# A GRU scan with an expert-choice layer: bias into the sum banks by ScalarE, six banks for late sums, exponentials in an odd step

## The chip, the cores and the metric

The kernel runs on one core of a Trainium2 chip. The metric is the device time of one execution in microseconds; lower is better. TensorE (PE) does matmuls into PSUM, VectorE (DVE) and ScalarE (ACT) do elementwise work, GpSimd (POOL) copies in SBUF, and SyncE (SP) issues DMAs. [...]

## What is computed

Sixteen sequences of 256 steps with 512 features go through a GRU, one step after another. The hidden states of all 4096 tokens then go through a layer in which each of 16 experts picks its 256 best tokens; all experts share one weight matrix, so a token's output is its sum `h @ expert_w + expert_b` times the sum of the weights with which experts picked it.

```python
r = sigmoid(x @ W_ir + b + h @ W_hr + b');  z = sigmoid(...)
n = tanh(x @ W_in + b + r * (h @ W_hn + b'));  h = (1 - z) * n + z * h      # 256 steps
S = softmax(hs @ router_w + router_b)                                       # 16 experts
G, idx = top_k(S.T, 256)                                                    # per expert
y = zeros.at[idx].add(G[..., None] * (hs[idx] @ expert_w + expert_b))
out = x + y
```

## The kernel before

**Groups.** Tokens are held in 32 groups of 128 (8 steps x 16 sequences). The expert's sums of 15 early groups (0, 1, 2, and those from 4 to 27 with g % 4 < 2) are made inside the scan; those of the 17 late groups at its end and behind it.

**The scan.** `for s in range(T)` issues each step by hand (manual schedule: every engine runs its list in the order in which the code issues it). TensorE's order in a step is `h_part` for r, n, r, n, z (L458, 96 matmul records), `x_part` for the next pair of steps (L445; 24 records in even steps, 40 in odd ones), and then fillers: one *unit* of an early group's sums (`expert`, L407, four matmuls), or in two steps of every 32 the router's logits. ScalarE runs r's sigmoid (L516), two tanhs (L569), z's sigmoid zs (L570) and, in even steps alone, copies that preset the next pair's gate banks with the bias: `preset_first` (L422) right behind r, `preset_rest` (L425, at times L429, L433) behind zs. VectorE has the rest of the chain, ending in the new state hs (L590), which the next step's h_part waits for.

**Sum banks.** `ps_m` has two banks. An early group's bank is taken in `expert` at its first unit; the first of its matmuls has `start=True`, and `expert_done` (L419) adds the bias `eb` as VectorE copies the sums to SBUF, a half in each of the next two steps. Unit n runs in step n + 8, so groups begin in steps 8, 24, 40, ... 232. `idle` is one more tile of `ps_m`; `keep_clock` writes zeros into it at the kernel's start, and `begin_sums` (L112) is the four zero matmuls of one bank.

**Late sums.** `late_items` are 16 whole late groups and two halves of the last one, numbered 0 to 17 here. `late_begin` (L160) takes a bank for an item and lets ScalarE copy the bias into it; the matmuls (L137) add to that. In steps 250 and 252 (T - 6, T - 4) it begins items 0 and 1 with `fresh=True`: zero matmuls first. Item i + 2 begins when item i's matmuls have been issued; of five banks in turn, two are from `ps_m` and three from `ps_e`. `expert_for(n)` issues n parts of this work between other TensorE work.

**Softmax.** Behind the sums for step s = T - 16 = 240 to 243 come four stages for the 28 groups whose logits are done: the exponential on ScalarE (L388, with a table load before it, and a small sigmoid, L627, to load the old table again), a reduction (L390), a reciprocal (L392) and a product (L395) on VectorE.

**The tail.** Logits are transposed into `ps`; `by_bits` then looks for each expert's threshold bit by bit: VectorE counts (L658), TensorE sums the counts into `counts` (L673), VectorE decides (L676, L681). 17 bits, each with three parts of late sums on TensorE. Then `pg` (L701) sums the weights of picked tokens, `gate` (L705) is copied out, and `store` (L711, L714) scales each group's sums, adds x and issues the output's DMA, early groups first, then the late items. From the gate on (`gated`) late sums stay in their banks until their store reads them; items 0 to 7 have been copied to SBUF by then (L178). Near the end a check counts again (L780, L783).

Of the kernel before, what the change touches and what calls it, by code (L numbers as in the profile page):

```python
# [8 lines left out]
F32 = mybir.dt.float32  # L9
# [4 lines left out]
ALU = mybir.AluOpType  # L14
# [4 lines left out]
def kernel(  # L19
# [34 lines left out]
    nc = tc.nc  # L54
    B, T, D = x.shape
# [96 lines left out]
    late_done = []  # L152
    gated = []

    def late_begin(pool, fresh=False):
        g, cols = late_items[len(late_done) + len(late)]
        pe = pool.tile([P, D], F32, name="pe", tag="pe")
        if fresh:
            begin_sums(pe)
        nc.scalar.copy(pe[:, cols], eb[:, cols])  # L160
        late.append(pe)

    def late_parts():
        for i, (g, cols) in enumerate(late_items):
            pe = late[0]
            for k in range(KC):

                for part in [cols] if gated or cols != whole else halves_d:
                    late_part(g, pe, k, part)
                    if k == KC - 1 and part.stop == cols.stop:  # L170
                        if i + 2 < len(late_items):
                            late_begin(ps_m if (i + 2) % 5 < 2 else late_pool[0])
                        late.pop(0)
                        late_done.append((g, cols))
                        if gated:
                            late_sums[g, cols.start] = pe
                        else:
                            nc.scalar.copy(wide(g), pe)  # L178
                    yield
# [9 lines left out]
    with (  # L189
# [206 lines left out]

        pes = {}

        def expert(g, unit):


            quarter, k = divmod(unit, KC)
            if unit == 0:
                pes[g] = ps_m.tile([P, D], F32, name="pe", tag="pe")
            at = P * quarter
            for j in range(KC):
                nc.tensor.matmul(  # L407
                    pes[g][quadrant(j), at : at + P],
                    ht[:, g, k, quadrant(j)],
                    ewr[:, k, E + P * quarter : E + P * (quarter + 1)],  # L410
                    start=(k == 0),
                    stop=(k == KC - 1),
                    tile_position=(0, QD * j),
                )

        def expert_done(g, half):
            d = slice(HD * half, HD * (half + 1))
            to = xs[:, NG - 4, :] if g == 0 else wide(g)
            nc.vector.tensor_tensor(to[:, d], pes[g][:, d], eb[:, d], ALU.add)  # L419

        def preset_first(p):
            nc.scalar.copy(ra[p % 2], bias[:, 0:2, :])  # L422
# [42 lines left out]
                        skip_group_check=True,  # L465
                    )

        idle = ps_m.tile([P, D], F32, name="idle", tag="pe")

        def keep_clock(n):  # L470

            for _ in range(n):
                begin_sums(idle)

        with tc.manual_schedule(engines={ET.PE, ET.DVE}):
            for bank in banks:
# [23 lines left out]
        with tc.manual_schedule(engines={ET.PE, ET.Activation, ET.DVE, ET.Pool, ET.SP}):  # L500
# [4 lines left out]
            for s in range(T):  # L505
# [28 lines left out]
                if apart:  # L534
                    logits(hn[(p + 1) % 2][:, P:], (2 * c, 2 * c + 1), range(g - KC, g))
                else:
                    while units and n_units - len(units) < s - TG + 1:
                        g_, unit = units.pop(0)
                        expert(g_, unit)
                        if unit == 15:  # L540
                            done += [(g_, 0), (g_, 1)]
                if s == T - 2:
                    logits(hn[0][:, P:], range(KC), range(NG - KC, NG - 1))
                if s == T - 1:
# [60 lines left out]
                        nc.gpsimd.tensor_copy(wide(0), xs[:, NG - 4, :])  # L605
                if taken:
                    expert_done(*taken)
                if c == 3 and g + 1 < NG:
                    turn_x(g + 1, xa_next)

# [8 lines left out]
                if s == T - 2:  # L619
                    gather(NG - 1)  # L620
                if s in (T - 6, T - 4):
                    late_begin(ps_m, fresh=True)
                if T - 16 <= s < T - 12:
                    softmax(slice(0, NG - KC), s - (T - 16))
                    if s == T - 16:

                        nc.scalar.activation(seen[0:1, 0:1], seen[0:1, 0:1], AF.Sigmoid)  # L627

# [10 lines left out]
    with (  # L639
        tc.tile_pool(name="route", bufs=1) as rt,  # L640
        tc.tile_pool(name="work", bufs=2) as wk,
        tc.tile_pool(name="ps_s", bufs=1, space=bass.MemoryType.PSUM) as ps_s,
        tc.tile_pool(name="ps_c", bufs=1, space=bass.MemoryType.PSUM) as ps_c,
        tc.tile_pool(name="ps_n", bufs=1, space=bass.MemoryType.PSUM) as ps_n,
        tc.tile_pool(name="ps_e", bufs=3, space=bass.MemoryType.PSUM) as ps_e,
    ):
        late_pool.append(ps_e)
        sT = rt.tile([P, QG * P], F32, name="sT")
# [75 lines left out]
            nc.gpsimd.memset(order[:, i : i + 1], float(i + 1))  # L724

        with tc.manual_schedule(engines={ET.PE, ET.Activation, ET.DVE}):
            ps = ps_s.tile([P, KC, P], F32, name="ps", tag="s")
            ps_last = ps_n.tile([P, P], F32, name="ps_last", tag="n")
            lg_f = lg.rearrange("p e g -> p (e g)")
            for c in range(KC - 1):  # L730
                nc.tensor.transpose(ps[:, c, :], lg_f[:, c :: KC], ident)
            nc.tensor.transpose(ps_last, lg_f[:, KC - 1 :: KC], ident)
            by_block = sT.rearrange("p (q c i) -> p c q i", q=QG, c=KC)
            nc.scalar.copy(by_block[:, 0 : KC - 1], ps[:, 0 : KC - 1, :].rearrange("p c (q i) -> p c q i", q=QG))
            nc.vector.tensor_copy(by_block[:, KC - 1], ps_last.rearrange("p (q i) -> p q i", q=QG))

            expert_for(2)
            counts = ps_c.tile([P, HIGH - LOW + 1], F32, name="counts")
            top = by_bits(KNOWN, HIGH, LOW, counts, lambda bit: expert_for(3))


            nc.vector.scalar_tensor_tensor(at_least, sT, top.bitcast(F32), sT, ALU.is_le, ALU.mult)
            most = rt.tile([P, NTOP], F32, name="most")
            nc.vector.max(out=most, in_=at_least)
            spread = rt.tile([P, GH, NTOP], F32, name="spread")
            nc.vector.tensor_tensor(
                spread,
                row_of.unsqueeze(2).to_broadcast([P, GH, NTOP]),
                most.unsqueeze(1).to_broadcast([P, GH, NTOP]),
                ALU.mult,  # L750
            )
            expert_for(2)
            all_most = ps_n.tile([P, GH * NTOP], F32, name="all_most", tag="n")
            nc.tensor.matmul(all_most, same_f, spread.rearrange("p h n -> p (h n)"), start=True, stop=True)
            expert_for(3)
            room = above(counts)
            nc.vector.max(out=most, in_=all_most)
            kth = rt.tile([P, 1], F32, name="kth")
            nc.vector.scalar_tensor_tensor(
                order, order, room, most, ALU.is_equal, ALU.mult, accum_out=kth  # L760
            )
            pg = ps_s.tile([P, QG, GH], F32, name="pg", tag="s")
            for q in range(QG):
                part = slice(q * P, (q + 1) * P)
                nc.vector.scalar_tensor_tensor(at_least[:, part], sT[:, part], kth, sT[:, part], ALU.is_ge, ALU.mult)
                sum_weights(q, pg)
                if q % 2:
                    expert_for(1)
            gate = gate_of(pg)

            gated.append(True)
            items = [(g, whole) for g in early_groups] + late_items
            for i, (g, cols) in enumerate(items):
                while g in late_groups and (g, cols) not in late_done:
                    expert_for(1)

                step = i - (len(items) - 6)
                if step == 1:
                    n = ps_n.tile([P, 1], F32, name="n", tag="n")
                    nc.tensor.matmul(n, same_h, cnt, start=True, stop=True)  # L780
                elif step == 2:
                    n_wrong = ps_n.tile([1, 1], F32, name="n_wrong", tag="n")
                    nc.tensor.matmul(n_wrong, wrong, wrong, start=True, stop=True)  # L783
                store(g, late_sums.get((g, cols.start), wide(g)), gate, cols)
                if step == 0:
                    cnt = count(kth, "cnt")
                elif step == 1:
                    wrong = wk.tile([P, 1], F16, name="wrong")
                    nc.vector.tensor_scalar(wrong, n, float(TOPK), None, ALU.not_equal)
                elif step == 2:  # L790
                    nc.vector.tensor_copy(flag, n_wrong)

        again = nc.values_load(flag, min_val=0, max_val=P)
        with tc.If(again > 0):
# [14 lines left out]
            for g in range(NG):  # L809
                nc.sync.dma_start(out=xs[:, g, :], in_=x[:, g * TG : (g + 1) * TG, :])  # L810

            counts = ps_c.tile([P, 30], F32, name="counts")
            kth = by_bits(0, 29, 0, counts, lambda bit: None).bitcast(F32)


# [23 lines left out]
            nc.vector.tensor_tensor(  # L839
                rank, rank, last.unsqueeze(2).to_broadcast([P, B, QG * TG]), ALU.is_le  # L840
            )
            pg = ps_s.tile([P, QG, GH], F32, name="pg", tag="s")
            for q in range(QG):
                nc.vector.tensor_tensor(
                    by_row(at_least)[:, :, q, :], by_step(rank)[:, :, q, :], by_row(at_least)[:, :, q, :], ALU.mult
# [42 lines left out]
```

## Time and profile before

| | |
|---|---|
| median of 3 runs | 1164.77 us (1163.73 to 1165.15) |
| the profiled execution | 1164.63 us, its span 1162.8 us |
| scan: first to last r | 25.3 to 1088.0 us |
| search for the thresholds | 1094.7 to 1121.0 us |
| gate known, stores | 1126.6 to 1158.1 us |
| last output packets | between 1159 and 1160 us |
| granted TensorE clock | 1.00 from 20 us to the last matmul (0.97 from 20 to 25) |

How to read it: the scan is a fixed chain of 256 steps, so a step's time is the distance between the starts of two rows of r. In a timeline's row, the first number is the start, the second the length, both in us from the span's start; in brackets is the idle time of the engine before it, and what the profile takes for its end. Matmul records overlap, since four 32-row blocks run side by side, and "PE busy" says only that something was in flight; the rows of weight loads (PEld) show the cadence at which TensorE's list moves.

### The profile page before, as it was taken

What the parts mean: (1) busy time and instruction counts of PE and PEld (TensorE: products, weight loads), DVE (VectorE), ACT (ScalarE), POOL (GpSimd) and SP (SyncE); (2) the same over time, 40 slices, a digit from 0 to 9 for tenths busy, and PEclk for the clock granted to TensorE, in tenths of its full rate; (3) what the DMA queues carried; (4) which work ended last, traced back from release to release, by engine and by line L of the source; (5) the groups of instructions that cost most, each with busy time, mean ns of one, the idle gap of its engine ahead of it and who ended that gap; (6) DMA issues with size and microseconds to landing.
All of it is one profiled execution on the core that took longest, in us unless ns stands there. A gap on an engine that the chain in (4) does not pass through costs nothing. (4 is left out here: it accounts for less than half of the span.)

```text
span 1162.8 us, 79365 instructions
## 1 busy us (share of the span) xinstructions
PE 1147.7 (99%) x36025; PEld 1018.4 (88%) x36025; DVE 703.6 (61%) x4078; ACT 336.1 (29%) x1444; POOL 100.0 (9%) x412
## 2 busy tenths in 40 slices
PE   7999999999999999999999999999999999999998
PEld 4899999999999999999999999999999999989742
DVE  1656665666666666666665666666656666665675
ACT  0323223232323232323232322332223222243320
POOL 3000010000000000000000000000000000000000
PEclk8999999999999999999999999999999999999999
DMA  7200000000000000000000000000000000000017
GB/s 231 76 23 20 21 18 22 21 19 19 20 21 20 21 20 21 20 21 21 20 20 21 21 20 18 22 21 20 18 23 20 21 18 23 20 16 14 3 54 240
DMA packets 48854, 38.01 MB, mean 33 GB/s; under 512 B 7968, under 2 KB 40800, under 8 KB 48512
## 3 DMA queue, kind: packets, MB, share of 16 engines
q1 hardware_dynamic: 46272, 29.56, 8.7%
q8 instruction: 283, 4.64, 1.6%
q10 hardware_dynamic: 1632, 3.15, 0.8%
q14 instruction: 59, 0.48, 0.1%
q0 software_dynamic: 608, 0.19, 0.1%
HBM read 24.47 MB, written 8.39 MB: 28 GB/s over the span
## 5 line engine op out<-in xcount | busy, mean ns | idle before, releaser
L458 PE MATMUL gates<-whh,hs 128*16 128x128 f32 x24576 | 723.2, 273 | 3.4 <-DVE hs L590 3.3
L458 PEld LDWEIGHTS gates<-whh,hs 128*16 128x16 f32 x24576 | 675.6, 103 | 9.5 <-DVE hs L590 4.1
L445 PE MATMUL gates<-wih,xt 128*32 128x256 f32 (+1 forms) x8192 | 385.7, 327 | 4.0 <-DVE xt L258 4.0
L445 PEld LDWEIGHTS gates<-wih,xt 128*32 128x32 f32 x8192 | 256.0, 110 | 65.9 <-DVE xt L258 4.3
L516 ACT ACTIVATE r<-gates 128x128 f32<-128x128 f32 x256 | 71.1, 278 | 614.1 <-PE gates L458 614.1
L520 DVE COPY seen<-r 1x1 f32<-1x1 f32 x256 | 36.3, 142 | 330.2 <-ACT r L516 330.2
L569 ACT ACTIVATE t<-t 128x64 f32<-128x64 f32 x512 | 102.9, 248 | 131.6 <-DVE t L567 131.6
L576 DVE STREAM_TRANSPOSE nT<-t 128x64 f32<-128x64 f32 x512 | 100.3, 234 | 49.0 <-ACT t L569 49.0
L579 DVE STREAM_TRANSPOSE zT<-zs 128x64 f32<-128x64 f32 x512 | 121.6, 237 | 0.2 <-issue 0.2
L590 DVE TENSOR_TENSOR hs<-v,nT 128x32 f32<-128x32 f32 x512 | 101.6, 198 | 21.7
L587 DVE TENSOR_TENSOR v<-u,zT 128x32 f32<-128x32 f32 x512 | 104.5, 204 | 8.8
L407 PE MATMUL pe<-ewr,ht 128*32 128x128 f32 x1920 | 97.0, 273 | 0.0
L565 DVE TENSOR_TENSOR t<-r,gates 128x64 f32<-128x64 f32 x512 | 89.7, 217 | 0.0
L567 DVE TENSOR_TENSOR t<-t,gates 128x64 f32<-128x64 f32 x512 | 88.4, 214 | 0.0
L407 PEld LDWEIGHTS pe<-ewr,ht 128*32 128x32 f32 x1920 | 63.6, 110 | 17.4
L582 DVE TENSOR_TENSOR u<-hs,nT 128x32 f32<-128x32 f32 x512 | 78.3, 153 | 0.0
L570 ACT ACTIVATE zs<-gates 128x128 f32<-128x128 f32 x256 | 71.0, 277 | 0.0
L137 PE MATMUL pe<-ewr,ht 128*32 128x256 f32 (+1 forms) x848 | 64.5, 442 | 0.5 <-ACT pe L160 0.5
L617 POOL COPY xa<-hs 32x1 f32<-32x1 f32 x120 | 21.4, 179 | 478.2 <-DVE hs L590 297.4
L333 POOL COPY ht<-hs 128x128 f32<-128x128 f32 (+1 forms) x128 | 46.8, 396 | 160.9 <-DVE hs L590 153.1
L249 POOL COPY xs<-hs 1x1 f32<-1x1 f32 x128 | 22.7, 178 | 338.5 <-DVE hs L590 333.5
L137 PEld LDWEIGHTS pe<-ewr,ht 128*32 128x32 f32 x848 | 25.9, 109 | 27.0 <-issue 16.8
(102 smaller groups left out, 310.1 us busy)
## 6 DMA issues: line engine op xcount, KB each, us to landing
xs<-in_x_dram SPq DMA_DIRECT2D x128, 64.0 KB
xa<-in_x_dram SPq DMA_DIRECT2D x248, 32.0 KB
out_dram<-xs SPq DMA_DIRECT2D x31, 256.0 KB
wih<-in_L_cond_W_ih_dram SPq DMA_DIRECT2D x3, 512.0 KB
wih<-in_L_cond_W_ih_dram ACTq DMA_DIRECT2D x3, 512.0 KB
whh<-in_L_cond_W_hh_dram SPq DMA_DIRECT2D x3, 512.0 KB
whh<-in_L_cond_W_hh_dram ACTq DMA_DIRECT2D x3, 512.0 KB
ewr<-in_L_ffn_expert_w_dram SPq DMA_DIRECT2D x1, 1024.0 KB
```

The lines of the kernel that those rows point to most:

```text
L137: nc.tensor.matmul(pe[q, cols], ht[:, g, k, q], ewr[:, k, E:][:, cols], start=False, stop=(k == KC - 1), tile_position=(0, QD * j), skip_g ...
L407: nc.tensor.matmul(pes[g][quadrant(j), at : at + P], ht[:, g, k, quadrant(j)], ewr[:, k, E + P * quarter : E + P * (quarter + 1)], start=( ...
L445: nc.tensor.matmul(dst, lhs, rhs, start=False, stop=(k == KC - 1), tile_position=(0, QD * j), skip_group_check=True)
L458: nc.tensor.matmul(dst[quadrant(j, m)], lhs, columns(whh[:, k, gate_, :], j), start=False, stop=(k == KC - 1), tile_position=(0, QD * j), ...
L565: nc.vector.tensor_tensor(t[half], r[:, cols], hn[p % 2][:, cols], ALU.mult)
L567: nc.vector.tensor_tensor(t[half], t[half], ra[p % 2][:, 1, cols], ALU.add)
L569: nc.scalar.activation(t[half], t[half], AF.Tanh)
L576: nc.vector.transpose(nT[half], t[half])
L579: nc.vector.transpose(zT[half], zs[:, halves[half][1]])
L582: nc.vector.tensor_tensor(u[half], hs[:, halves[half][2], slot(s), :], of_step(nT[half], odd), ALU.subtract)
L587: nc.vector.tensor_tensor(v[half], u[half], of_step(zT[half], odd), ALU.mult)
L590: nc.vector.tensor_tensor(hs[:, halves[half][2], slot(s + 1), :], v[half], of_step(nT[half], odd), ALU.add)
```

## The change

Four parts:

1. An early group's bank is taken at the end of the step before its first unit, by `expert_begin`: ScalarE copies the bias into it. The group's matmuls then all add (`start=False`), and `expert_done` is a copy without the bias. The expert's loop leaves a step after a group's last unit. `keep_clock` writes its zeros to two tiles in turn, so that both banks of `ps_m` have been written by TensorE.
2. `late_begin` has no zero matmuls any more.
3. `counts` and `pg` move into the bank of the transposes (`bank`), the pool `ps_c` goes, and `ps_e` has four banks: late items take six banks in turn.
4. The four softmax stages of 28 groups run in steps T - 15 to T - 12 (241 to 244).

```diff
-    def late_begin(pool, fresh=False):
+    def late_begin(pool):
...
-        if fresh:
-            begin_sums(pe)
         nc.scalar.copy(pe[:, cols], eb[:, cols])
...
-                            late_begin(ps_m if (i + 2) % 5 < 2 else late_pool[0])
+                            late_begin(ps_m if (i + 2) % 6 < 2 else late_pool[0])
...
+        def expert_begin(g):
+            pes[g] = ps_m.tile([P, D], F32, name="pe", tag="pe")
+            nc.scalar.copy(pes[g], eb)
...
-            if unit == 0:
-                pes[g] = ps_m.tile([P, D], F32, name="pe", tag="pe")
...
-                    start=(k == 0),
+                    start=False,
...
-            nc.vector.tensor_tensor(to[:, d], pes[g][:, d], eb[:, d], ALU.add)
+            nc.vector.tensor_copy(to[:, d], pes[g][:, d])
...
-        idle = ps_m.tile([P, D], F32, name="idle", tag="pe")
+        idles = [ps_m.tile([P, D], F32, name="idle", tag="pe") for _ in range(2)]
...
-            for _ in range(n):
-                begin_sums(idle)
+            for i in range(n):
+                begin_sums(idles[i % 2])
...
                         if unit == 15:
                             done += [(g_, 0), (g_, 1)]
+                            break
...
                 if taken:
                     expert_done(*taken)
+
+                if units and units[0][1] == 0 and units[0][0] not in pes and s >= TG - 1:
+                    expert_begin(units[0][0])
...
                 if s in (T - 6, T - 4):
-                    late_begin(ps_m, fresh=True)
-                if T - 16 <= s < T - 12:
-                    softmax(slice(0, NG - KC), s - (T - 16))
-                    if s == T - 16:
+                    late_begin(ps_m)
+                if T - 15 <= s < T - 11:
+                    softmax(slice(0, NG - KC), s - (T - 15))
+                    if s == T - 15:
...
-        tc.tile_pool(name="ps_c", bufs=1, space=bass.MemoryType.PSUM) as ps_c,
...
-        tc.tile_pool(name="ps_e", bufs=3, space=bass.MemoryType.PSUM) as ps_e,
+        tc.tile_pool(name="ps_e", bufs=4, space=bass.MemoryType.PSUM) as ps_e,
...
-            ps = ps_s.tile([P, KC, P], F32, name="ps", tag="s")
+            bank = ps_s.tile([P, D], F32, name="bank", tag="s")
+            ps = bank[:, 0 : (KC - 1) * P].rearrange("p (c d) -> p c d", d=P)
+            by_counts = lambda n: bank[:, (KC - 1) * P : (KC - 1) * P + n]
+            pg = bank[:, 0 : QG * GH].rearrange("p (q h) -> p q h", h=GH)
...
-            counts = ps_c.tile([P, HIGH - LOW + 1], F32, name="counts")
+            counts = by_counts(HIGH - LOW + 1)
```

More of the change, by code (lines that the diff above doesn't have):

```diff
@@ L410, in expert @@
                     ewr[:, k, E + P * quarter : E + P * (quarter + 1)],
-                    start=(k == 0),
+                    start=False,
                     stop=(k == KC - 1),
                     tile_position=(0, QD * j),
+                    skip_group_check=True,
                 )
@@ L761 @@
             )
-            pg = ps_s.tile([P, QG, GH], F32, name="pg", tag="s")
             for q in range(QG):
@@ L810 @@
                 nc.sync.dma_start(out=xs[:, g, :], in_=x[:, g * TG : (g + 1) * TG, :])
-            counts = ps_c.tile([P, 30], F32, name="counts")
+            counts = by_counts(30)
             kth = by_bits(0, 29, 0, counts, lambda bit: None).bitcast(F32)
@@ L841 @@
             )
-            pg = ps_s.tile([P, QG, GH], F32, name="pg", tag="s")
             for q in range(QG):
```

## The prediction, made before the changed kernel ran

> **What bounds the kernel now.** I read the page first: TensorE is busy over the whole span, so the question is in which stages its queue really is the limit.
>
> ```profile
> span 1162.8 us, 79365 instructions
> PE 1147.7 (99%) x36025; PEld 1018.4 (88%) x36025; DVE 703.6 (61%) x4078; ACT 336.1 (29%) x1444; POOL 100.0 (9%) x412
> ```
>
> Second, the timeline of ScalarE: the start of the r sigmoid (L516) is the clock of the scan, one row a step. Steps 208 to 212, then 240 to 244 with the moved exponential (L388) between:
>
> ```profile
> 892.04 0.28 ACT L516 ACTIVATE r<-gates 128x128 f32<-128x128 f32 x1 [2.62 <-PE gates L458]
> 896.12 0.28 ACT L516 ACTIVATE r<-gates 128x128 f32<-128x128 f32 x1 [1.88 <-PE gates L458]
> 900.26 0.28 ACT L516 ACTIVATE r<-gates 128x128 f32<-128x128 f32 x1 [2.56 <-PE gates L458]
> 904.39 0.28 ACT L516 ACTIVATE r<-gates 128x128 f32<-128x128 f32 x1 [2.19 <-PE gates L458]
> 908.60 0.28 ACT L516 ACTIVATE r<-gates 128x128 f32<-128x128 f32 x1 [2.62 <-PE gates L458]
> ...
> 1025.57 0.28 ACT L516 ACTIVATE r<-gates 128x128 f32<-128x128 f32 x1 [2.62 <-PE gates L458]
> 1027.78 1.28 ACT L388 ACT_TABLE_LOAD   x1
> 1029.07 0.58 ACT L388 ACTIVATE lg<-lg 128x448 f32<-128x448 f32 x1
> 1029.65 1.28 ACT L627 ACT_TABLE_LOAD   x1
> 1030.95 0.20 ACT L627 ACTIVATE seen<-seen 1x1 f32<-1x1 f32 x1
> 1031.06 0.25 ACT L516 ACTIVATE r<-gates 128x128 f32<-128x128 f32 x1
> ...
> 1043.24 0.28 ACT L516 ACTIVATE r<-gates 128x128 f32<-128x128 f32 x1 [2.62 <-PE gates L458]
> ```
>
> An undisturbed block of four steps takes 908.60 - 892.04 = 16.56 us and repeats to 0.01 us: TensorE's filler (x_part, one expert unit) just covers the chain of sigmoid, tanh and transposes. The block with the exponential takes 17.67, so it loses 1.11.
>
> Third, steps without expert units, early and late in the scan:
>
> ```profile
> 33.31 0.28 ACT L516 ACTIVATE r<-gates 128x128 f32<-128x128 f32 x1 [2.42 <-PE gates L458]
> 37.21 0.28 ACT L516 ACTIVATE r<-gates 128x128 f32<-128x128 f32 x1 [2.01 <-PE gates L458]
> 41.21 0.28 ACT L516 ACTIVATE r<-gates 128x128 f32<-128x128 f32 x1 [2.42 <-PE gates L458]
> ...
> 1067.78 0.28 ACT L516 ACTIVATE r<-gates 128x128 f32<-128x128 f32 x1 [2.42 <-PE gates L458]
> 1071.85 0.28 ACT L516 ACTIVATE r<-gates 128x128 f32<-128x128 f32 x1 [0.74 <-PE gates L458]
> ```
>
> Without filler the chain alone needs 3.90 us from an even to an odd step and 4.00 from odd to even. With it, steps take 4.08 to 4.20. The cover is therefore only some 0.2 us a step, either way: anything that delays r by more than that is lost time.
>
> Fourth, the timeline of the tail, where stores wait for late sums:
>
> ```profile
> 1142.62 2.35 ACT L160 COPY pe<-eb 128x512 f32<-128x512 f32 x4 [16.12 <-DVE xs L711]
> 1143.26 0.16 PEld L137 LDWEIGHTS pe<-ewr,ht 128*32 128x32 f32 x8 [1.40 <-ACT pe L160]
> 1143.27 3.64 PE L137 MATMUL pe<-ewr,ht 128*32 128x512 f32 x32 [0.49 <-ACT pe L160]
> ...
> 1150.41 7.08 PE L137 MATMUL pe<-ewr,ht 128*32 128x512 f32 x96
> 1157.63 0.48 DVE L711 SCALAR_TENSOR_TENSOR xs<-pe,gate,xs 128x256 f32<-128x256 f32 x1 [1.24 <-DMA out_dram<-xs]
> ```
>
> The stores of the 23 groups whose sums already lie in SBUF end at 1142 us, and only then does bank after bank come free. TensorE had run five late items ahead, one a bank, and stood. After 1143.27 it never stops until 1157.49 (1150.41 + 7.08); the last store follows at once. The last row names a DMA, but it starts 0.14 after TensorE's end, and in the table by stretches the DMA engines are 7% busy from 1154 to 1155 and idle from 1155 to 1156. So the end is set by TensorE's stream, not by the output's bytes.
>
> **The change part by part.**
>
> *Exponentials in step 241 instead of 240.* From the first table load to the next r is 31.06 - 27.78 = 3.28 us in ScalarE's queue, and that stays. What goes is what stood before it: in an even step zs is followed by three copies (L425, L429, L433), which an odd step hasn't. In odd step 243, zs starts 1.31 after r and takes 0.28, so the load would start at r + 1.59. r of step 241 falls, undisturbed, at 1025.57 + 4.08 = 1029.65; the load at 1031.24, r of step 242 at 1034.52. Undisturbed it would come 4.14 after, at 1033.79: 0.73 late. The cover in an even step is 4.13 - 3.90 = 0.23, which leaves a loss of 0.50 against 1.11: gain 0.61, taken as 0.60. Bounds: 0.38 if nothing covers, 1.11 if all is covered. Behind r wait its preset copy (L422, done 0.55 after r's start) and x_part on TensorE, which is held some 0.4 us; the late chain holds h_part longer in the same step, so it isn't added.
>
> The three VectorE stages move one step too. The reduction (0.99 us) goes to an even step's end, where VectorE idles about 1.3 before seen. The reciprocal (0.32) now follows turn_x in step 243, where 0.49 idle is left in such a step; before, the product (0.58) stood there. The product goes to step 244, with 1.3 idle. Without that cover they would cost their excess, under 0.3 in all.
>
> [...]
>
> *No zeroing in steps 250 and 252.* Four zero matmuls stand ahead of the next h_part on TensorE twice. The interval is 71.85 - 67.78 = 4.07 against 3.90 without filler: 0.17 each, gain 0.34. The bound below is 0.20, by the interval from 1059.80 to 1063.77 (3.97) in which only VectorE had more to do. The bias copies no longer wait for the zeroing; ScalarE is idle anyway.
>
> *Six banks.* Until the gated items nothing moves: ScalarE frees the banks early. Then TensorE has one more bank, for the item that it stood for. Weight loads come every 0.43 us, in fours; the one at 1143.26 waited 1.40 where a steady one waits 0.30, but the first matmuls of an item normally follow their load by 0.43 and here by 0.01. So the stall is 1.40 - 0.30 - 0.43 = 0.67. Bounds: 0.49 (the idle time in the matmul row) and 1.10 (the whole wait of the loads). The next item's bank is stored from 1141.84 and refilled by 1143.2; TensorE needs it 3.4 us after 1142.6, at 1146.0, so no new bank wait. Before that item TensorE has the check's count matmul (L780), whose count VectorE ends at 1145.89 (its row: 1145.13 + 0.74, then the accumulator's read): in time by 0.1.
>
> *Counts and gate sums in the transposes' bank.* The same instructions, and in the program's order a counts matmul waits for VectorE alone, as before. Zero, within 17 x 0.05 us if a wait crept in.
>
> *Bias by ScalarE.* 15 new copies of 128x512 at the end of steps 7, 23, ... 231: 15 x 0.594 (L160) = 8.9 us, all in the 2.6 us that ScalarE idles before an even step's r; the bank's last reader was done over ten steps earlier, and eb's load is issued at 39 us against 55 for the first copy. TensorE's expert matmuls keep number and shape. 30 VectorE adds of 0.418 become copies; the nearest copy from PSUM (L481, 128x256) takes 0.425, so +0.2 in all, in idle time of 1.5 a step. The break changes no step, since each group ends with a step of one unit. The second idle bank adds no matmul.
>
> *A side effect on ScalarE's instruction stream.* At step 52 r starts 0.321 us after its sequencer wait ended instead of 0.045; the same at steps 116 and 180, exactly 384 ScalarE instructions apart. At 52 the two intervals are 4.48 and 3.88 instead of 4.20 and 4.07: 0.09 lost, three times 0.27. [...] Gain 0.27; bound the other way -0.27. [...]
>
> Sum: 0.60 + 0.34 + 0.67 + 0.27 = 1.88 us, within 0.80 (0.38 + 0.20 + 0.49 - 0.27) and 2.82 (1.11 + 0.34 + 1.10 + 0.27). The profiled execution took 1164.63 us around its span of 1162.8, 0.14 under the median of 1164.77. So: span 1160.9, that execution 1162.75, median 1162.9.
>
> **The rivals.**
>
> *Everything at its upper end.* The exponentials hide wholly and the tail recovers the whole wait of the loads: 1164.77 - 2.82 = 1161.95. For it: cover and bank are really there. Against: 3.28 us is more than the 2.9 between zs and r in an odd step.
>
> *The freed wait comes back at L780.* The count hangs on VectorE's stores, paced at 0.66 us from the gate on; my margin is 0.1. If TensorE waits there or at the next bank for the 0.67, what is left is 1.21: 1163.6.
>
> *Slower: the bias copies in ScalarE's queue.* If a copy can't start when it stands at the head (its bank not free, or TensorE's older work still pending on it), r queues behind it. It decides from a copy that ends 2.6 us late or more. If each of 15 pushed r by its own 0.59, less 0.23 cover, that is +5.4, less 1.88: 1168.3. Against: its bank is long free in the trace.
>
> *Nothing measurable.* The scan's filler takes up each gain and the end is the output's after all: 1164.8. Against: the idle DMA at 1155.
>
> **How the numbers follow.** Forecast 0.52, upper end 0.22, wait at L780 0.15, nothing 0.04, slower 0.07. A measurement can tell about 0.2%, 2.3 us, from no change: below 1162.4 counts as faster, above 1167.1 as slower. The upper end is faster and so is the fringe of the forecast (0.02): 0.24; slower 0.07; within 0.69. The range runs from the upper end, 1161.9, to 1165.0, which takes in the L780 case and no change with the runs' own spread (up to 1165.15).
>
> **What would show it.** Right: r of step 242 about 4.9 after r of 241 and four steps from 240 in 17.05; 3.90 from r of 250 to r of 251; no ScalarE copy that waits for a store ahead of the sixth gated item's matmuls, TensorE unbroken from the gate to its last matmul; r of step 52 4.2 after 51. Wrong: r late at steps 8, 24, 40, ...; a gap before L780's successor of over 0.3; output DMA busy without pause to the end.

## The result and the profile after

| | before | after |
|---|---|---|
| median, lowest to highest (20 runs each) | 1164.79 us, 1163.73 to 1166.32 | 1162.82 us, 1161.82 to 1163.48 |
| the profiled execution, its span | 1164.63, 1162.8 us | 1162.40, 1160.5 us |

The ratio is 0.9983, with a 95% interval from 0.9977 to 0.999: 1.97 us by the medians, where 1.9 had been forecast. Every term of the sum can be found in the trace after. The page's head (busy time, share and instructions of each engine) first:

```profile
span 1160.5 us, 79363 instructions
PE 1145.6 (99%) x36017; PEld 1008.8 (87%) x36017; DVE 703.4 (61%) x4078; ACT 343.2 (30%) x1459; POOL 100.0 (9%) x412
```

Eight matmuls are gone (the two zeroings), ScalarE has 15 instructions more (the copies; 7.1 us of busy time, since each begins 0.1 before the row of zs ends), VectorE is as it was. None of this says where the time went; the starts of r do.

**The exponentials.** ScalarE's timeline from step 240 to step 244 (start, length, engine, line; in brackets the idle time before). r is now L517, exp L386, the small sigmoid L632:

```profile
1024.98 0.28 ACT L517 ACTIVATE r<-gates 128x128 f32<-128x128 f32 x1 [2.62 <-PE gates L459]
...
1029.06 0.28 ACT L517 ACTIVATE r<-gates 128x128 f32<-128x128 f32 x1 [1.88 <-PE gates L459]
...
1030.37 0.28 ACT L572 ACTIVATE zs<-gates 128x128 f32<-128x128 f32 x1
1030.66 1.28 ACT L386 ACT_TABLE_LOAD   x1
1031.96 0.58 ACT L386 ACTIVATE lg<-lg 128x448 f32<-128x448 f32 x1
1032.54 1.28 ACT L632 ACT_TABLE_LOAD   x1
1033.84 0.20 ACT L632 ACTIVATE seen<-seen 1x1 f32<-1x1 f32 x1
1033.94 0.25 ACT L517 ACTIVATE r<-gates 128x128 f32<-128x128 f32 x1
...
1037.80 0.28 ACT L517 ACTIVATE r<-gates 128x128 f32<-128x128 f32 x1 [2.08 <-PE gates L459]
...
1042.01 0.28 ACT L517 ACTIVATE r<-gates 128x128 f32<-128x128 f32 x1 [2.62 <-PE gates L459]
```

The load follows zs at once, 1.60 after r of step 241; r of 242 is the only row of r without idle time before it, so ScalarE's own queue holds it, and it comes 1033.94 - 1029.06 = 4.88 after r of 241. The four steps take 1042.01 - 1024.98 = 17.03.

**The steps without zeroing, and one of the three stalls.** ScalarE's timeline again, first at steps 250 and 251, where item 0's bias copy (L158) now follows the preset copies, then at 51 to 53:

```profile
1066.54 0.28 ACT L517 ACTIVATE r<-gates 128x128 f32<-128x128 f32 x1 [2.42 <-PE gates L459]
...
1068.36 0.59 ACT L158 COPY pe<-eb 128x512 f32<-128x512 f32 x1
1070.44 0.28 ACT L517 ACTIVATE r<-gates 128x128 f32<-128x128 f32 x1 [1.50 <-PE gates L459]
```

```profile
236.20 0.28 ACT L517 ACTIVATE r<-gates 128x128 f32<-128x128 f32 x1 [2.19 <-PE gates L459]
...
240.40 0.28 ACT L517 ACTIVATE r<-gates 128x128 f32<-128x128 f32 x1 [2.62 <-PE gates L459]
...
244.48 0.28 ACT L517 ACTIVATE r<-gates 128x128 f32<-128x128 f32 x1 [2.19 <-PE gates L459]
```

1070.44 - 1066.54 is 3.90, the bare chain. Step 51 to 52 takes 4.20 and 52 to 53 4.08, where it had been 4.48 and 3.88. The same three rows of the kernel before:

```profile
236.52 0.28 ACT L516 ACTIVATE r<-gates 128x128 f32<-128x128 f32 x1 [2.19 <-PE gates L458]
...
241.00 0.28 ACT L516 ACTIVATE r<-gates 128x128 f32<-128x128 f32 x1 [2.89 <-PE gates L458]
...
244.88 0.28 ACT L516 ACTIVATE r<-gates 128x128 f32<-128x128 f32 x1 [2.08 <-PE gates L458]
```

Steps 116 and 180 changed in the same way.

**The tail.** The timeline of all engines, from the gate to the last store (VectorE's rows show each store):

```profile
1123.45 2.15 ACT L158 COPY pe<-eb 128x512 f32<-128x512 f32 x4
...
1124.84 19.95 PE L137 MATMUL pe<-ewr,ht 128*32 128x256 f32 x192
...
1141.20 1.69 ACT L158 COPY pe<-eb 128x512 f32<-128x512 f32 x3 [15.61 <-DVE xs L715]
...
1144.72 0.18 PE L787 MATMUL n<-cnt,same_h 128*128 128x1 f16 x1
1144.83 3.64 PE L137 MATMUL pe<-ewr,ht 128*32 128x512 f32 x32
1148.29 0.17 PE L790 MATMUL n_wrong<-wrong 128*1 128x1 f16 x1
1148.29 7.08 PE L137 MATMUL pe<-ewr,ht 128*32 128x512 f32 x96
...
1155.51 0.48 DVE L715 SCALAR_TENSOR_TENSOR xs<-pe,gate,xs 128x256 f32<-128x256 f32 x1 [1.24 <-DMA out_dram<-xs]
```

The bias copies of 1123.45 now include the sixth gated item's bank, some 16 us before the stores free the first one (1141.20). TensorE goes through 1141 without a stop, and nothing waits at the check's count (L787): the next item's first matmul starts 0.11 behind it. TensorE's last matmul ends 68.76 us after the last r, where it had been 69.45; the last store starts 68.90 after it instead of 69.60.

### The profile page after: what moved, and what is told of

Same layout as the page of the kernel before. It is cut to its first block, busy times and chain, and to the rows that moved or that the text cites. A ratio compares the mean times of both kernels' runs of the same rounds, so it can differ in the third digit from the quotient of the medians.

```text
span 1160.5 us, 79363 instructions
## 1 busy us (share of the span) xinstructions
PE 1145.6 (99%) x36017; PEld 1008.8 (87%) x36017; DVE 703.4 (61%) x4078; ACT 343.2 (30%) x1459; POOL 100.0 (9%) x412
## 3 DMA queue, kind: packets, MB, share of 16 engines
q8 instruction: 283, 4.64, 1.7%
## 5 line engine op out<-in xcount | busy, mean ns | idle before, releaser
L459 PE MATMUL gates<-whh,hs 128*16 128x128 f32 x24576 | 719.4, 273 | 3.5 <-DVE hs L592 2.0
L459 PEld LDWEIGHTS gates<-whh,hs 128*16 128x16 f32 x24576 | 672.2, 103 | 10.0 <-DVE hs L592 4.6
L446 PE MATMUL gates<-wih,xt 128*32 128x256 f32 (+1 forms) x8192 | 380.9, 327 | 4.4 <-DVE xt L256 4.3
L446 PEld LDWEIGHTS gates<-wih,xt 128*32 128x32 f32 x8192 | 245.2, 110 | 72.4 <-DVE xt L256 4.6
L517 ACT ACTIVATE r<-gates 128x128 f32<-128x128 f32 x256 | 70.9, 277 | 605.5 <-PE gates L459 605.5
L407 PE MATMUL pe<-ewr,ht 128*32 128x128 f32 x1920 | 93.9, 273 | 0.0
L407 PEld LDWEIGHTS pe<-ewr,ht 128*32 128x32 f32 x1920 | 59.5, 110 | 19.4
L137 PEld LDWEIGHTS pe<-ewr,ht 128*32 128x32 f32 x848 | 26.0, 109 | 26.2 <-issue 17.4
```

Of the source, the lines that this page charges most:

```text
L137: nc.tensor.matmul(pe[q, cols], ht[:, g, k, q], ewr[:, k, E:][:, cols], start=False, stop=(k == KC - 1), tile_position=(0, QD * j), skip_g ...
L407: nc.tensor.matmul(pes[g][quadrant(j), at : at + P], ht[:, g, k, quadrant(j)], ewr[:, k, E + P * quarter : E + P * (quarter + 1)], start=F ...
L446: nc.tensor.matmul(dst, lhs, rhs, start=False, stop=(k == KC - 1), tile_position=(0, QD * j), skip_group_check=True)
L459: nc.tensor.matmul(dst[quadrant(j, m)], lhs, columns(whh[:, k, gate_, :], j), start=False, stop=(k == KC - 1), tile_position=(0, QD * j), ...
```

## The experiments

Since the whole change is worth 0.17%, one part can hardly be told from the spread by its time alone. So each kernel was profiled too, and its r's compared step by step with those of its parent: outside the steps named below, and the step from 254 to 255, which is treated at the end, all of them repeat to 0.01 to 0.06 us behind step 10. The first ten steps don't: r of step 0 came between 24.3 and 25.9 us in these traces, of kernels that hardly differ up to there. All effects in the scan are therefore counted from r of step 10, and those of the tail from r of step 255. In the table, "us" is the median of 10 or 11 runs (of 4 for the six copies), and before is the median of 15 to 33 runs of the kernel before, taken on the same chip along with them. The medians alone don't add up at this size: the first three rows, each with one part of the change, are 1.19, 0.64 and 0.79 below before, 2.62 in sum, against 1.97 for the whole change. So the size of each part is read from the traces.

| kernel | us | before | ratio, 95% interval |
|---|---|---|---|
| before + exponentials in an odd step | 1163.20 | 1164.39 | 0.9989, 0.9980 to 0.9998 |
| before + six banks | 1163.75 | 1164.39 | 0.9992, 0.9983 to 1.0001 |
| before + bias by ScalarE | 1163.60 | 1164.39 | 0.9992, 0.9983 to 1.0001 |
| before + one small instruction | 1164.24 | 1164.39 | 0.9997, 0.9987 to 1.0006 |
| after + zeroing | 1162.81 | 1164.63 | 0.9988, 0.9979 to 0.9997 |
| after without the exponentials | 1161.69 | 1164.63 | 0.9975, 0.9966 to 0.9985 |
| after, two units put off | 1162.48 | 1164.63 | 0.9981, 0.9972 to 0.9990 |
| after, three units put off | 1162.77 | 1164.63 | 0.9983, 0.9974 to 0.9992 |
| after + three small instructions | 1162.81 | 1164.00 | 0.9987, 0.9978 to 0.9996 |
| after, bias copied three times | 1162.71 | 1164.00 | 0.9985, 0.9976 to 0.9994 |
| after, bias copied six times | 1174.81 | 1164.00 | 1.0089, 1.0074 to 1.0104 |
| after, two useful units put off, list shifted | 1162.05 | 1164.37 | 0.9979, 0.9970 to 0.9988 |

**One part alone: the exponentials.**

```diff
-                if T - 16 <= s < T - 12:
-                    softmax(slice(0, NG - KC), s - (T - 16))
-                    if s == T - 16:
+                if T - 15 <= s < T - 11:
+                    softmax(slice(0, NG - KC), s - (T - 15))
+                    if s == T - 15:
```

> The kernel before with only the exponentials moved to step 241. Theory (the load starts behind zs alone, and the scan's 0.2 us of cover takes part of what is left): four intervals of r from step 240 sum to 17.0 us instead of 17.67, r of 242 comes 4.9 after r of 241, the time falls by 0.6 us. Rival A (the loads cost what they cost, wherever they stand): 17.67 and no change. Rival B (all hidden): 16.56 and -1.1 us. r of 52, 116 and 180 stay 0.28 late, 250 to 251 stays 4.07, the tail after the last r stays 69.6 us to the last store.

The four intervals sum to 17.03, r of 242 comes 4.89 after r of 241; 52, 116, 180, 250 and the tail (69.6) are as before. So this part gives 17.67 - 17.03 = 0.64, and neither rival holds.

**One part alone: six banks.**

```diff
-                            late_begin(ps_m if (i + 2) % 5 < 2 else late_pool[0])
+                            late_begin(ps_m if (i + 2) % 6 < 2 else late_pool[0])
...
-        tc.tile_pool(name="ps_c", bufs=1, space=bass.MemoryType.PSUM) as ps_c,
...
-        tc.tile_pool(name="ps_e", bufs=3, space=bass.MemoryType.PSUM) as ps_e,
+        tc.tile_pool(name="ps_e", bufs=4, space=bass.MemoryType.PSUM) as ps_e,
```

(and the counts and gate sums in the transposes' bank, as in the change)

> The kernel before with only the sixth bank (and the counts and gate sums in the transposes' bank). Theory (one stall of TensorE on a bank goes and nothing takes its place): from the last r to the last store 0.7 us less (68.9 instead of 69.6), the time -0.7 us. Rival (the wait comes back at the check's count or at a later bank): 69.6 and no change, with a gap in TensorE's late items at another place. If the extra 0.15 us of step 254 in the kernel after comes from the tail's rearrangement, r of 255 is 4.25 after r of 254 here; if not, 4.10.

TensorE's timeline from the gate on, first in the kernel with five banks (that of the part before), then with six:

```profile
1125.04 16.52 PE L137 MATMUL pe<-ewr,ht 128*32 128x256 f32 x160
1142.05 3.64 PE L137 MATMUL pe<-ewr,ht 128*32 128x512 f32 x32 [0.49 <-ACT pe L160]
```

```profile
1126.69 19.95 PE L137 MATMUL pe<-ewr,ht 128*32 128x256 f32 x192
1146.58 0.18 PE L781 MATMUL n<-cnt,same_h 128*128 128x1 f16 x1
1146.68 3.64 PE L137 MATMUL pe<-ewr,ht 128*32 128x512 f32 x32
```

The 0.49 of idle time on a bias copy is gone, and no other took its place. The last store starts 68.91 after the last r instead of 69.60: 0.69. r of 255 is 4.10 behind r of 254, so the tail's new order is not what lengthens that step in the kernel after.

**One part alone: bias by ScalarE.**

```diff
+        def expert_begin(g):
+            pes[g] = ps_m.tile([P, D], F32, name="pe", tag="pe")
+            nc.scalar.copy(pes[g], eb)
...
-                    start=(k == 0),
+                    start=False,
...
-            nc.vector.tensor_tensor(to[:, d], pes[g][:, d], eb[:, d], ALU.add)
+            nc.vector.tensor_copy(to[:, d], pes[g][:, d])
```

(with its call, the break and the two idle banks, as in the change; the zeroing stays)

> The kernel before with only the bias put into the early groups' banks by ScalarE (copies of eb, matmuls that add, plain copies out, the two idle banks, the break). Theory (the copies lie in ScalarE's idle time; their only effect is that the list of ScalarE's instructions is shifted): r of 52, 116 and 180 no longer late, steps 8, 24, ... as before, -0.27 us. Rival A (copies push r): r of 8, 24, ..., 232 late by up to 0.6 each, +5.4 us. Rival B (neither): the three stalls stay or move to other steps, 0.

r of 52, 116 and 180 comes 0.28 earlier in its step, and the next step gives 0.19 back: three times 0.09. No step 8, 24, ... changes. Rival A and rival B both fall.

**A shift of ScalarE's list and nothing else.** One instruction more, in the kernel before:

```diff
+                if s == 9:
+                    for _ in range(1):
+                        nc.scalar.activation(seen[0:1, 0:1], seen[0:1, 0:1], AF.Sigmoid)
```

> The kernel before with one more 1x1 sigmoid on ScalarE at the end of step 9, nothing else. Theory (the stalls of 0.28 us at 52, 116 and 180 belong to places in ScalarE's list of instructions, 128 apart, and show where such a place falls between the wait for r's banks and r): shifted by one, they are gone at all three, the intervals from 51 to 53 fall from 8.36 to 8.27, -0.27 us in all. Rival (something of those steps themselves, such as a transfer): stalls stay at 52, 116 and 180, no change.

The same three stalls vanish, 0.279 in each and 0.19 given back. ScalarE's timeline at step 52:

```profile
240.97 0.28 ACT L516 ACTIVATE r<-gates 128x128 f32<-128x128 f32 x1 [2.61 <-PE gates L458]
```

So all that the bias by ScalarE brings, it brings by shifting the list. The other direction, three instructions more in the kernel after (the same lines with `range(3)`):

> The kernel after with three 1x1 sigmoids on ScalarE at the end of step 9. Theory (places 128 apart in ScalarE's list of instructions): counted out, two of the places fall between the wait and r, at steps 30 and 220, and no other: r is 0.28 late there and nowhere else, +0.18 us in all. Rival (the stalls of before belong to steps 52, 116 and 180): none, or stalls at those steps.

```profile
148.53 0.28 ACT L517 ACTIVATE r<-gates 128x128 f32<-128x128 f32 x1 [2.89 <-PE gates L459]
```

That is r of step 30, with 2.89 idle before it in place of 2.62. It is 0.276 late, r of 220 0.279, and 0.19 is given back each time; no other step from 12 to 254 moved. The sum is 0.17.

**The zeroing put back.**

```diff
-    def late_begin(pool):
+    def late_begin(pool, fresh=False):
...
+        if fresh:
+            begin_sums(pe)
         nc.scalar.copy(pe[:, cols], eb[:, cols])
...
-                    late_begin(ps_m)
+                    late_begin(ps_m, fresh=True)
```

> The kernel after with the zeroing of the two banks of steps 250 and 252 put back, nothing else. Theory (four zero matmuls ahead of h_part lengthen each of two steps by 0.17 us): 250 to 251 and 252 to 253 take 4.07 instead of 3.90, +0.34 us. Rival (the steps were only rearranged, the time is given back in the tail): the intervals grow but the end stays, 0. The step from r of 254 to r of 255 (4.25 in the kernel after, 4.10 before) falls back to 4.10 if the zero matmuls' absence, by its shift of TensorE's list, makes it; then the sum is only +0.19.

Both intervals are 4.07 again (+0.17 each), and the step from 254 to 255 falls from 4.25 to 4.10 (-0.14): +0.20 in the trace. By the time alone the difference from the kernel after can't be seen. So leaving out the zeros gave 0.34 and cost 0.14 in another step.

**The exponentials left out.**

```diff
-                    softmax(slice(0, NG - KC), s - (T - 15))
-                    if s == T - 15:
-                        nc.scalar.activation(seen[0:1, 0:1], seen[0:1, 0:1], AF.Sigmoid)
+                    if s > T - 15:
+                        softmax(slice(0, NG - KC), s - (T - 15))
```

> The kernel after without the exponentials of the first 28 groups and without the two table loads around them in step 241 (the weights of these groups are then no softmax). Theory (the exponentials still cost what the cover doesn't take): four intervals from 240 sum to 16.56 instead of 17.03, -0.47 us. Rival (the loss is already hidden): no change.

The block is 16.56: r of 242 is 0.744 earlier, and 0.276 of that is lost again in the next step. The loss of 0.47 is real, and it is all that this stage still costs.

**How much fits behind zs.** The bias copies three times over, and in a second kernel six times (`range(6)`):

```diff
-            nc.scalar.copy(pes[g], eb)
+            for _ in range(3):
+                nc.scalar.copy(pes[g], eb)
```

> The kernel after with each bias copy done three times over (same bank, same values). Theory (an odd step leaves ScalarE 2.6 us behind zs before the next r; three copies take 1.8): r of 8, 24, ..., 232 on time, 0 us apart from two places in the instruction list that now fall before r (30 and 218, 0.09 each). Rival (any copy there pushes r, or one is free and more are not): 15 x 0.6 to 1.2, +9 us or more.

> The kernel after with each bias copy done six times over. Theory (six take 3.5 us, about 1.0 more than there is room for; the scan covers 0.2): r of 8, 24, ... 1.0 late, some 0.75 us lost at each of 15 steps, +11 us. Rival A (ScalarE's queue has more room than that): 0. Rival B (no cover at all): +15 us.

Steps 23 and 24 in ScalarE's timeline, in the kernel after and with six copies:

```profile
120.69 0.59 ACT L399 COPY pe<-eb 128x512 f32<-128x512 f32 x1
123.41 0.28 ACT L517 ACTIVATE r<-gates 128x128 f32<-128x128 f32 x1 [2.13 <-PE gates L459]
```

```profile
122.98 3.70 ACT L400 COPY pe<-eb 128x512 f32<-128x512 f32 x6
126.62 0.27 ACT L518 ACTIVATE r<-gates 128x128 f32<-128x128 f32 x1
```

There are 123.41 - 120.69 = 2.72 us from the first copy to r. Three copies take 1.84, and r of 8, 24, ... isn't late (0.06 early, which the next step gives back); r is late at 30 and at 218 alone (0.276 and 0.277), where the places of the list had been counted out, and an r late by 0.28 shows in the same way at 70 and at 252 with six. Six take 3.70; r has no idle time before it and comes 0.917 late at each of these steps, and only 0.126 is given back: 15 x 0.79 = 11.9 us, and the medians are 1174.81 - 1162.82 = 12.0 apart. So the rival that ended slower was a real mechanism with its point at 2.7 us, and one copy stands 2.1 us away from it.

**Filling the shadow of the table loads.** Weight loads in the kernel after show TensorE idle for 0.35 us before x_part of step 242 (L446) and for 0.25 before h_part of step 243 (L459):

```profile
1034.51 1.02 PEld L446 LDWEIGHTS gates<-wih,xt 128*32 128x32 f32 x24 [0.35 <-ACT gates L423]
...
1036.22 2.56 PEld L459 LDWEIGHTS gates<-whh,hs 128*32 128x32 f32 x96 [0.25 <-DVE hs L592]
```

Units of early groups can be put off into that, two of them or, with `{T - 18: 1, T - 17: 2, T - 16: 3}`, three:

```diff
+            behind = {T - 17: 1, T - 16: 2}
...
-                    while units and n_units - len(units) < s - TG + 1:
+                    while units and n_units - len(units) < s - TG + 1 - behind.get(s, 0):
```

> The kernel after with the expert units of steps 239 and 240 put off to step 241, where TensorE waits for r of 242. Theory (TensorE idles 0.34 + 0.26 us in the shadow of the table loads, a unit takes 0.22 of it, and a step without its unit is 0.18 to 0.2 shorter): 239 to 241 shorter by 0.35 in sum, r of 242 still 4.9 after r of 241, h_part of 243 no later: -0.35 us against the kernel after. Rival (two more units ahead of h_part delay r of 242 as much as they save): no change.

> As the version with two units put off, with those of steps 238, 239 and 240 in step 241, four units there. Theory (0.66 us of units against 0.60 of idle time): -0.5 us against the kernel after, h_part of 243 up to 0.06 later. Rival (r of 242 is pushed by what is too much): r of 242 5.1 or more after r of 241, and no better than with two.

Neither did what was expected. With two, r of 240 comes 0.158 earlier, but step 240 without its unit is as long as with it (4.08): half of the gain. In that trace the step from 254 to 255 happens to be 0.17 longer than in the kernel after, so from step 10 to step 255 nothing is left of it. With three, r of 239 and of 240 come 0.171 and 0.156 earlier, step 240 again brings nothing, and 242 to 243 grows by 0.19, though r of 242 is still 4.885 behind r of 241: the third extra unit is one too many, but the price is paid a step later than the rival had it. In step 240 VectorE's second transposition of zs, which the new state needs, starts 2.55 us after r, against 2.18 in step 238. Just before it VectorE is idle for 0.22, which the profile puts to no engine (here with two units put off):

```profile
1027.38 0.24 DVE L582 STREAM_TRANSPOSE zT<-zs 128x64 f32<-128x64 f32 x1 [0.22 <-issue]
```

All 14 traces have it at 2.55, the kernel before too. That step 240 is the first of a group of eight is not the reason: 224, 232 and 248 are such steps as well, and have 2.25. What it has in common with the late r's on ScalarE is its place: among VectorE's rows it is 63 behind a multiple of 128, and an 8 KB packet of the profile's queue q14, kind "instruction", starts 0.65 to 0.67 us after it (see the last section). Other VectorE rows with that place show no delay of this size, and no run shifts VectorE's list, so this cause is possible but not shown.

**What step 254 lost, and a better version.** By now the interval from r of 254 to r of 255 had been 4.10 in all six kernels with the zeroing, and 4.22 to 4.43 in the seven without. The last run puts off only the two units that pay, and adds eight zero matmuls at the start, where TensorE has to wait for x anyway (r of step 0 came at 25.56, within the spread of 24.3 to 25.9):

```diff
-            keep_clock(22)
+            keep_clock(24)
...
+            behind = {T - 18: 1, T - 17: 2, T - 16: 2}
```

(with the condition of the loop as above)

> The kernel after with two edits. First, the expert units of steps 238 and 239 are put off to step 241 (three units there); step 240 keeps its one, because without it r of 241 came no earlier. Second, two more groups of four zero matmuls at the start, where TensorE waits 4.57 us for x: they set every later TensorE instruction back by 16 places in its list, to where it stood in the kernel before. [...] Together -0.48 us, 1162.3. Rivals: if the extra in step 254 is made by the missing zero matmuls in steps 250 and 252 in another way than by places in the list, it stays and only -0.33 is left; if three units in step 241 are too many, the interval from 242 to 243 grows by 0.19, as with four, and nothing is left of the first part's gain but 0.14.

Weight loads of step 254 (PEld), first in the kernel after, then in this one; the row is h_part of step 255, which waits for the new state:

```profile
1084.97 2.12 PEld L459 LDWEIGHTS gates<-whh,hs 128*32 128x32 f32 x80 [0.60 <-issue]
```

```profile
1085.40 2.21 PEld L459 LDWEIGHTS gates<-whh,hs 128*32 128x32 f32 x81 [0.44 <-issue]
```

The step is 4.10 again, though the zeroing in 250 and 252 is still absent. The units put off are not what did it: with two and with three of them alone the step took 4.41 and 4.36. ScalarE's timeline, r of steps 238 to 243:

```profile
1017.64 0.28 ACT L518 ACTIVATE r<-gates 128x128 f32<-128x128 f32 x1 [2.62 <-PE gates L459]
...
1021.54 0.28 ACT L518 ACTIVATE r<-gates 128x128 f32<-128x128 f32 x1 [2.02 <-PE gates L459]
...
1025.59 0.28 ACT L518 ACTIVATE r<-gates 128x128 f32<-128x128 f32 x1 [2.46 <-PE gates L459]
...
1029.67 0.28 ACT L518 ACTIVATE r<-gates 128x128 f32<-128x128 f32 x1 [1.89 <-PE gates L459]
...
1034.56 0.25 ACT L518 ACTIVATE r<-gates 128x128 f32<-128x128 f32 x1
...
1038.41 0.28 ACT L518 ACTIVATE r<-gates 128x128 f32<-128x128 f32 x1 [2.08 <-PE gates L459]
```

238 to 239 takes 3.90 and 239 to 240 4.05 (4.07 and 4.20 in the kernel after), and the block from 240 stays 17.02. With the 0.15 of step 254 that is 0.171 + 0.156 + 0.147 = 0.47 less from step 10 to step 255, where 0.17 and 0.16 for r of 239 and 240 and 0.15 for step 254 had been expected, and the median of 1162.05 is the lowest of all kernels that compute everything. Against the kernel after it was not timed side by side; the two intervals against before (0.9970 to 0.9988 and 0.9977 to 0.9990) overlap, so the order of these two rests on the traces.

## Why the prediction was right

**Exponentials**: gain forecast 0.60, measured 0.64. r of 242 was to come "about 4.9" after r of 241 and came at 4.88; the forecast loss of 0.50 is 0.47. The one figure that was off is the cover: 0.23 was taken from an even step's 4.13 against the bare 3.90, and 0.276 was given back. The three VectorE stages cost nothing (243 to 244 and 244 to 245 unchanged).

**Zeroing**: forecast 0.34, measured 2 x 0.17. What the step left out is that removing eight matmuls also shifts TensorE's list; that took back 0.15 at step 254 in this trace, a term that the sum doesn't have. The same kind of side effect had been seen on ScalarE and counted out there, but not on TensorE.

**Six banks**: forecast 0.67, measured 0.69 to 0.70, by the part alone as in the whole. The reading that carried it was of weight loads: the idle time in the matmul row (0.49) alone would have been 0.2 short. The check's count, feared by a margin of 0.1, holds nothing up.

**Bias by ScalarE**: forecast zero for the copies, and zero it is, with room for three.

**ScalarE's list**: forecast 0.27, measured 3 x 0.09. The size is that of the three stalls in the trace before; that they would go was the author's estimate, which that trace doesn't show, and in the kernel after they are gone. Two kernels with nothing but a shift, one without the stalls and one with two at steps named beforehand (30 and 220, 0.276 and 0.279 late), show that the stalls go with places in the list.

**The sum**: 0.64 + 0.34 + 0.70 + 0.27 = 1.95, less 0.15 at step 254. The profiled spans differ by 2.23 (unrounded) instead of 1.8, for two reasons outside the change: r of step 10 came 0.36 earlier, which is within the first steps' spread, and from the last matmul to the end it took 5.16 instead of 5.27, where the other kernels' traces lie between 5.17 and 5.37. By the medians, forecast and result agree within 0.1 us, which is less than the runs can tell. That they agree so closely is in part luck: by the traces it is 1.80. The four parts brought 0.07 more than forecast, and a step that had not been thought of took back 0.15, where other kernels with that list lost between 0.12 and 0.33.

**The rivals**: the upper end falls with the exponentials left out (0.47 was still there to gain); the wait at the count falls with the tail's 0.7; no measurable effect falls with the interval of the ratio; the slower one was priced at 0.36 net a copy, and where it was made to happen, a step lost 0.79 of 0.92, since steps 8, 24, ... give back 0.13 and not 0.23.

## What to carry to other kernels

In a long chain of equal steps, compare the starts of one instruction step by step: intervals that repeat to 0.01 us show effects of 0.1 us, which the 10 to 20 timed runs of a kernel here could not, and every odd step is a question worth asking. A gain of such a size can come from an edit's side effect on where instructions stand in an engine's list (three times 0.09 us here, by one small instruction alone), so run the edit's shift alone before crediting the edit. Cover differed from step to step here (0.13 us behind steps 8, 24, ... with six copies, 0.19 behind 52, 116 and 180, 0.276 behind 242): measure it in the very step that is to be lengthened.

## What was not expected of the hardware

In these traces an instruction starts late at certain places of an engine's list. On ScalarE this was r, by 0.276 to 0.279 us in eight places of four kernels (three of before, two with three small instructions, two with three copies, one with six) and by 0.29 in a ninth, in step 252, all of them whole multiples of 128 instructions apart within a kernel. In most even steps the wait ahead of r is an instruction of its own in the trace. In the nine places r starts 0.32 to 0.34 us after that wait has ended; in the other such steps of all 14 traces it starts within 0.05. The two kernels that keep before's list, those with the exponentials or the six banks alone, stall in its three places too.

Counted in ScalarE's rows, waits included, r of all nine stands 63 behind a multiple of 128 (rows 319, 703 and 1087 in the kernel before, the first row being 0), and no r of an even step stands there without being late. In odd steps r carries its wait itself, and there r at the same place is on time: 73, 137, 201 and 243 in the kernel with one small instruction, 51 with three, 151 with six copies. So the place of r alone doesn't make it late: in the nine, the wait is 62 behind a multiple of 128 and r 63. Packets of one queue come at the same times. The page of the kernel before has a queue q14, kind "instruction", with 59 packets and 0.48 MB in the span, 8 KB each. One of them starts 0.64 to 0.69 us after r in each of the nine places (0.66, 0.67 and 0.66 in the kernel before), and in the kernel after none starts near r of 52, 116 and 180. What holds r up the traces don't show.

TensorE has late starts at places of its list too, of another size. The count goes by the trace's rows again (a float32 matmul of the program is two weight loads and two matmuls there, a zero matmul one of each), here with the first row as place 1. By it the wait ahead of h_part of step 255 stands at place 70097 of the list in the kernels that have the eight zero matmuls or make up for them, and at 70081, one behind a multiple of 128 counted from place 64, in those that don't. In all 14 traces this wait ends 2.41 us after r of 254. The weight load behind it starts 0.02 to 0.03 us later in the seven of the first kind, and 0.16 to 0.37 later in the seven of the second. The step's extra was zero in the first kind and between 0.12 and 0.33 in the second, where it varied from trace to trace. A queue q8, kind "instruction" as well, has packets of 16 KB (283 and 4.64 MB in the kernel after). One of them starts 3.68 us after r of 254 in the kernel after, behind the late load, but 1.85 after it in the kernel before and 1.70 in the last version, ahead of the wait's end. Whether waits at nearby places would be followed by late loads too was not tried; what makes the load late and why the size varies is open.
